# Moving a GRU state's transposes from TensorE to the DMA engines, with four groups of graphs under way

## The chip, the cores and the metric

One core of one Trainium2 chip. The metric is device time in microseconds (us), from the first to the last instruction of the kernel, of the slowest (here the only) core. The kernel before takes 2229.0 us (median of three runs, 2228.56 to 2229.5). The engines: TensorE (PE for matmuls, PEld for loading their stationary operand), VectorE (DVE), ScalarE (ACT), GpSimd (POOL) and SyncE (SP), whose queue issues all of the data transfers here.

## What is computed

128 graphs of 128 nodes with 256 features (`x`), and their adjacency (`adj`, about one edge in eight). Layer 0 is a gated graph network of three steps, layer 1 a graph attention; both stand behind a layer norm with ReLU and are added to their input.

```python
# layer 0
h = relu(layernorm(x))
A = (adj != 0)
for i in range(3):
    m    = h @ weight[i]
    aggr = einsum('bst,bsd->btd', A, m)            # sums over edges
    gi, gh = aggr @ w_ih.T + b_ih, h @ w_hh.T + b_hh
    r, z = sigmoid(i_r + h_r), sigmoid(i_z + h_z)
    n    = tanh(i_n + r * h_n)
    h    = (1 - z) * n + z * h
x = x + h
# layer 1
h  = relu(layernorm(x))
Wh = h @ W
s  = Wh.sum(-1)
e  = leaky_relu(s[:, :, None] + s[:, None, :], 0.2)
e  = where(adj == 0, -inf, e)
x  = x + softmax(e) @ Wh
```

## The kernel before

The 128 graphs go through in 32 groups of four. The weight of the messages is folded into `w_ih` beforehand, so a step of a group needs two products: of the state, and of its sums over the edges. They run in fp32. Each product of 2x2 blocks is done with seven block products in place of eight (the sums of blocks that this takes are `node_sums`). The sums over edges multiply the state, split into three bf16 parts whose sum is the fp32 value, with the 0/1 matrix in bf16: three passes.

A group's state is needed in two layouts. `hT` (features on partitions) feeds the gate products and holds the state in steps 0 and 1; `rows` (nodes on partitions) feeds the sums over edges and, in step 2, the gates, which come out in rows. TensorE turns one into the other by transposes into PSUM, and ScalarE copies the result to SBUF:

```python
def rows_to_T(src, dst):                 # once per group
    for k in range(KD):
        ps = buf("misc")
        def turn(k=k, ps=ps):
            for b in range(G):
                nc.tensor.transpose(flat(ps)[:, b * N:(b + 1) * N],
                                    ap(src)[:, b, k * P:(k + 1) * P], ident)      # L472
        op("PE", 440, turn, [src], [ps], [dst])
        op("ACT", 590, ... nc.scalar.copy(ap(dst)[:, k, :], flat(ps)) ...)        # L475

def T_to_rows(src, dst):                 # after steps 0 and 1
    for n in range(2):
        ps = buf("misc")
        def turn(n=n, ps=ps):
            for b in range(2):
                for k in range(KD):
                    nc.tensor.transpose(ap(ps)[:, b, k * P:(k + 1) * P],
                                        ap(src)[:, k, ...], ident)                # L486
        op("PE", 440, turn, ...)
        op("ACT", 590, ... nc.scalar.copy(ap(dst)[:, 2 * n:2 * n + 2, :], ap(ps)) ...)  # L490

def edge_sums(rows, a, dst):
    r1, p3 = buf("r1"), buf("p3")
    for n in range(2):
        # top() is the upper half of each fp32 number, read in place as bf16
        op("POOL", ... r1 = rows - top(rows))                                     # L505
        op("POOL", ... p3 = r1 - top(r1), written as bf16)                        # L508
    for k in range(KD):
        ps = buf("misc")
        # 4 graphs x 3 parts, bf16 matmuls with a                                 # L517
        op("ACT", 590, ... copy to dst ...)                                       # L521
```

[...] The state update of steps 0 and 1, and the end of step 2:

```python
# gru: VectorE, two SBUF inputs each
d = hT - u;  d = d * z;  hT = u + d              # L679, L682, L684
# gru_rows
op("DVE",  690, ... d  = rows - u)               # L717
op("POOL", 1290, ... x1 = xt + u)                # L719
op("DVE",  690, ... d  = d * z)                  # L722
op("DVE",  690, ... x1 = x1 + d)                 # L724
```

[...] A group:

```python
def group(g):
    xt, at, a = buf("xt"), buf("at"), buf("a")           # loads of x and adj
    rows, hT = buf("rows"), buf("hT")
    normed(xt, rows)
    rows_to_T(rows, hT)
    for layer in range(L):
        hs, aT, gs = buf("hs"), buf("aT"), buf("gs")
        node_sums(hT, hs, "POOL", 1290, 780)             # L546 to L550
        edge_sums(rows, a, aT)
        node_sums(aT, gs, "DVE", 690, 422)
        plan.phase = phase(g, layer)                     # 3 * g + 2 * layer, but for the last groups
        if layer < L - 1:
            gru(layer, hT, hs, aT, gs)
            rows = buf("rows")
            T_to_rows(hT, rows)
    gru_rows(L - 1, hT, hs, aT, gs, rows, xt, x1)
    attention(g, a, x1, h1, ...)
```

[...] The kernel does not issue in this order. Every operation is entered in a `Plan` with its engine and an assumed duration; a list scheduler then plays the engines through and fixes the order of each engine's queue before anything runs on the chip. The gate products of all turns (a turn is one step of one group, in the order of `phase`) form a fixed chain on TensorE; other work fills in around it. Tiles are `"set"` (one per group under way, `SETS = 3`), `"turn"` (given out in the order of turns), `"free"` or `"all"`. The assumed durations settle only the order; they say nothing of the chip.

Of the kernel before, what the change touches and what calls it, by code (L numbers as in the profile page):

```python
# [10 lines left out]
I32 = mybir.dt.int32  # L11
AF = mybir.ActivationFunctionType
# [3 lines left out]
P = 128  # L16
G = 4
EPS = 1e-5
ALPHA = 0.2
SETS = 3  # L20
SLOT = 18150
MARGIN = 4000
# [4 lines left out]
class Buf:  # L27


    def __init__(self, tag, key, prev):  # L30
        self.tag, self.key, self.prev = tag, key, prev
        self.slot, self.accesses, self.left = None, [], 0


class Plan:
# [7 lines left out]
    LAG = {"PE": 250, "ACT": 300, "DVE": 300, "POOL": 300, "SP": 2500}  # L43
# [20 lines left out]
    def op(self, eng, ns, fn, reads=(), writes=(), room=(), due=None, mark=None,  # L64
           turn=None):
# [14 lines left out]
        for is_write, group in ((False, reads), (True, writes)):  # L80
            for item in group:
# [4 lines left out]
                for x in list(reads) + list(writes)}  # L86
        free = [b for b in bufs.values() if self.tags[b.tag][1] in ("free", "turn")]
        for b in free:
            b.left += 1
        self.nodes.append([eng, ns, fn, deps, free, self.due if due is None else due])  # L90
# [7 lines left out]
    def run(self):  # L98
# [6 lines left out]
        bound = set(chain)  # L105
        rank = [0] * len(nodes)
        for i in reversed(range(len(nodes))):
            eng, ns, due = nodes[i][0], nodes[i][1], nodes[i][5]
            gap = 0 if i in bound else MARGIN
            rank[i] = min([due] + [rank[u] - (0 if nodes[u][0] == eng else self.LAG[eng])  # L110
                                   - (gap if u in bound else 0) for u in users[i]]) - ns
        missing = [len(n[3]) for n in nodes]
        for i, mark in self.turns:
            if mark in self.marks:
                users[self.marks[mark]].append(i)
                missing[i] += 1
        ready = {e: [] for e in self.LAG}
        at = [0.0] * len(nodes)
        for i, n in enumerate(nodes):
            if not missing[i]:  # L120
                ready[n[0]].append(i)
        clock = dict.fromkeys(self.LAG, 0.0)
        slots = {t: [0.0] * n for t, (n, kind) in self.tags.items()
                 if kind in ("free", "turn")}
        waiting = {t: [b for _, _, b in sorted(w, key=lambda x: x[:2], reverse=True)]
                   for t, w in self.waiting.items()}
        order, end = [], 0.0
        while len(order) < len(nodes):
            best = None
            for e, pool in ready.items():  # L130
# [3 lines left out]
                for i in pool:  # L134
                    if i in bound and i != chain[-1]:
                        continue
                    t = max(clock[e], at[i])
                    for b in nodes[i][4]:
                        if b.slot is None:
                            t = max(t, min(slots[b.tag]))  # L140
                            if b.tag in waiting and waiting[b.tag][-1] is not b:
                                t = float("inf")
                    starts.append((t, i))
# [11 lines left out]
            clock[e] = t + n[1]  # L155
            end = max(end, clock[e])
            for b in n[4]:
# [6 lines left out]
                b.done = max(getattr(b, "done", 0.0), clock[e] + self.LAG[e])  # L164
                if not b.left:
                    slots[b.tag][b.slot[1]] = b.done
            for u in users[i]:
                missing[u] -= 1
                at[u] = max(at[u], clock[e] + (0 if nodes[u][0] == e else self.LAG[e]))
                if not missing[u]:  # L170
                    ready[nodes[u][0]].append(u)
# [6 lines left out]
def kernel(  # L178
# [37 lines left out]
        "xt": (3, "all", work, [P, G, D]), "at": (1, "all", work, [P, G, N]),  # L216
        "a": (4, "all", work, [P, G, N]),
        "r1": (2, "free", work, [P, G, D]), "p3": (2, "free", work, [P, G, D]),
        "hT": (1, "set", work, [P, KD, GN]), "rows": (1, "set", work, [P, G, D]),
        "hs": (1, "set", work, [P, 4, H]), "aT": (1, "set", work, [P, KD, GN]),  # L220
        "gs": (1, "set", work, [P, 4, H]),
        "st": (8, "all", work, [P, G, 6]), "mv": (8, "all", work, [P, G, 2]),
        "rs": (8, "all", work, [P, G]), "nm": (8, "all", work, [P, G]),
        "s": (2, "all", work, [P, G]), "top": (2, "all", work, [P, G]),
        "den": (2, "all", work, [P, G]), "rden": (2, "all", work, [P, G]),
# [7 lines left out]
        "u": (2, "free", work, [P, G * D]), "d": (2, "free", work, [P, GN]),  # L233
        "x1": (2, "all", work, [P, G, D]), "h1": (1, "all", work, [P, G, D]),
# [10 lines left out]
    DTYPE = {"at": I32, "a": BF16, "p3": BF16}  # L245
# [92 lines left out]
    def weights():  # L338
        plan.due, plan.phase = 10 ** 9, -1
        w_hh_nat, w_ih_nat = buf("rz"), buf("rz")  # L340
        w_msg = [buf("h1"), buf("h1")]

        def load_msg(layer):
            op("SP", 1300, lambda: nc.sync.dma_start(
                ap(w_msg[layer // 2])[:, 2 * (layer % 2):2 * (layer % 2) + 2, :],
                weight[layer].rearrange("(k p) e -> p k e", p=P)),
               [], [(w_msg[layer // 2], layer, layer + 1)])
# [8 lines left out]
        load_msg(2)  # L356
# [14 lines left out]
        homes = [[last("hs"), last("gs")], [last("aT"), last("rows")], [last("hT"), buf("xt")]]  # L371
        for layer in range(L):
# [3 lines left out]
            wT, half, msg = uT[layer // 2], layer % 2, w_msg[layer // 2]  # L376
            for e in range(KD):
                ps = bank(layer == 0)

                def turn(ps=ps, e=e, msg=msg, half=half):  # L380
                    for k in range(KD):
                        nc.tensor.transpose(flat(ps)[:, k * P:(k + 1) * P],
                                            ap(msg)[:, 2 * half + k, e * P:(e + 1) * P], ident)
                op("PE", 220, turn, [(msg, layer, layer + 1)], [ps])
                to_sbuf("ACT", D, ps, wT, half * GN + e * D)
            w_x = homes[layer]
# [91 lines left out]
    def T_to_rows(src, dst):  # L478

        for n in range(2):  # L480
            ps = buf("misc")

            def turn(n=n, ps=ps):
                for b in range(2):
                    for k in range(KD):
                        nc.tensor.transpose(ap(ps)[:, b, k * P:(k + 1) * P],  # L486
                                            ap(src)[:, k, (2 * n + b) * N:(2 * n + b + 1) * N],
                                            ident)
            op("PE", 440, turn, [(src, n, n + 1), (src, 2 + n, 3 + n)], [ps], [dst])
            op("ACT", 590, lambda n=n, ps=ps: nc.scalar.copy(  # L490
                ap(dst)[:, 2 * n:2 * n + 2, :], ap(ps)), [ps], [(dst, 2 * n, 2 * n + 2)])

# [5 lines left out]
    def edge_sums(rows, a, dst):  # L498

        r1, p3 = buf("r1"), buf("p3")
        for n in range(2):
            part = slice(2 * n, 2 * n + 2)
            op("POOL", 1290, lambda part=part: nc.gpsimd.tensor_tensor(  # L505
                ap(r1)[:, part], ap(rows)[:, part], top(rows)[:, part], OP.subtract),
               [(rows, 2 * n, 2 * n + 2)], [(r1, n, n + 1)])
            op("POOL", 1290, lambda part=part: nc.gpsimd.tensor_tensor(  # L508
                ap(p3)[:, part], ap(r1)[:, part], top(r1)[:, part], OP.subtract),
               [(r1, n, n + 1)], [(p3, n, n + 1)])  # L510
        for k in range(KD):
            ps = buf("misc")

            def edges(k=k, ps=ps):
                for b in range(G):
                    for i, m in enumerate((top(rows), top(r1), ap(p3))):
                        nc.tensor.matmul(flat(ps)[:, b * N:(b + 1) * N],  # L517
                                         m[:, b, k * P:(k + 1) * P], ap(a)[:, b, :],
                                         start=(i == 0), stop=(i == 2))
            op("PE", 700, edges, [rows, r1, p3, a], [ps], [dst])  # L520
# [19 lines left out]
    def node_sums(t, w, eng, cost, half):  # L540
# [3 lines left out]
        def blocks():  # L544
            return ap(t).rearrange("p k (n m) -> p (k n) m", n=2)
        op(eng, cost, lambda: sub(ap(w)[:, 0:2, :], blocks()[:, 1::2, :], blocks()[:, 0:2, :],  # L546
                                  OP.subtract), [t], [(w, 0, 2)])
        op(eng, half, lambda: sub(ap(w)[:, 2, :], ap(w)[:, 1, :], blocks()[:, 0, :], OP.add),
           [t, (w, 1, 2)], [(w, 2, 3)])
        op(eng, half, lambda: sub(ap(w)[:, 3, :], blocks()[:, 2, :], ap(w)[:, 2, :], OP.subtract),  # L550
           [t, (w, 2, 3)], [(w, 3, 4)])
# [98 lines left out]
    def gru(layer, hT, hs, aT, gs):  # L650
# [7 lines left out]
        for j, n, src in blocks:  # L658
# [7 lines left out]
                op0=OP.add, op1=OP.mult), [nn, (rz, i, i + 1), W["bias_h"]], [(u, i, i + 1)])  # L666
            op("DVE", 422, lambda j=j, n=n, nn=nn: nc.vector.tensor_tensor(  # L667
                view(u)[:, j, n, :], view(u)[:, j, n, :], ap(nn)[:, 1, :], OP.add),
               [nn], [(u, i, i + 1)])
# [3 lines left out]
        for j in (1, 0):  # L673
# [7 lines left out]
               [(hT, lo, hi), (u, lo, hi)], [d])  # L681
            op("DVE", 690, lambda d=d, cols=cols: nc.vector.tensor_tensor(  # L682
                ap(d), ap(d), ap(rz)[:, 1, cols], OP.mult), [(rz, 4 + lo, 4 + hi)], [d])
            op("DVE", 690, lambda j=j, d=d, cols=cols: nc.vector.tensor_tensor(  # L684
                ap(hT)[:, j, :], ap(u)[:, cols], ap(d), OP.add), [(u, lo, hi), d], [(hT, lo, hi)])

    def gru_rows(layer, hT, hs, aT, gs, rows, xt, x1):
# [6 lines left out]
        for j, n, src in blocks:  # L694
# [10 lines left out]
               [nn, (rz, i, i + 1)], [(u, i, i + 1)])  # L705
            op("DVE", 422, lambda outs=outs, graphs=graphs, nn=nn: nc.vector.tensor_tensor(
                view(u)[:, graphs, outs], view(u)[:, graphs, outs], ap(nn)[:, :, P:2 * P], OP.add),
               [nn], [(u, i, i + 1)])
        for n in (1, 0):
# [3 lines left out]
            def part(b, lo=lo, hi=hi):  # L713
# [4 lines left out]
                ap(d), part(rows), ap(u)[:, cols], OP.subtract), [(rows, lo, hi), (u, lo, hi)], [d])  # L718
            op("POOL", 1290, lambda cols=cols, part=part: nc.gpsimd.tensor_tensor(  # L719
                part(x1), part(xt), ap(u)[:, cols], OP.add),  # L720
               [(xt, lo, hi), (u, lo, hi)], [(x1, lo, hi)])
            op("DVE", 690, lambda d=d, cols=cols: nc.vector.tensor_tensor(  # L722
                ap(d), ap(d), ap(rz)[:, 1, cols], OP.mult), [(rz, 4 + lo, 4 + hi)], [d])
            op("DVE", 690, lambda d=d, part=part: nc.vector.tensor_tensor(  # L724
                part(x1), part(x1), ap(d), OP.add), [d], [(x1, lo, hi)])

    def phase(g, layer):


        late = int(g == NG - 2 and layer > 0) - int(g == NG - 1)  # L730
        return 3 * g + 2 * layer + late

    def group(g):
        graphs = slice(g * G, (g + 1) * G)
        plan.due = (3 * g - 1) * SLOT
        xt, at, a = buf("xt"), buf("at"), buf("a")
        op("SP", 1500, lambda: nc.sync.dma_start(ap(xt), x[graphs].rearrange("b n d -> n b d")),
           [], [xt])
        op("SP", 800, lambda: nc.sync.dma_start(ap(at), adj[graphs].rearrange("b n m -> n b m")),
# [3 lines left out]
        plan.due = (3 * g + 6) * SLOT  # L743
        rows, hT = buf("rows"), buf("hT")
        normed(xt, rows)
        rows_to_T(rows, hT)
        for layer in range(L):
            hs, aT, gs = buf("hs"), buf("aT"), buf("gs")
            node_sums(hT, hs, "POOL", 1290, 780)
            edge_sums(rows, a, aT)  # L750
            node_sums(aT, gs, "DVE", 690, 422)
            plan.phase = phase(g, layer)
            plan.cursor = plan.phase * SLOT
            if layer < L - 1:
                gru(layer, hT, hs, aT, gs)
                rows = buf("rows")
                T_to_rows(hT, rows)
        plan.due = (3 * g + 7) * SLOT
        x1, h1 = buf("x1"), buf("h1")
        gru_rows(L - 1, hT, hs, aT, gs, rows, xt, x1)  # L760
# [114 lines left out]
```

## Time and profile before

| | before |
|---|---|
| time, us | 2229.0 (2228.56 to 2229.5) |
| TensorE, granted clock | 0.995 |
| TensorE matmuls | 13414 |
| gate matmuls, two queue entries of 256 columns, mean ns | 379 to 386 |
| GpSimd: splitting into bf16 parts (L505, L508), us | 209.8 + 197.9 |
| ScalarE: copies behind transposes (L490, L475), us | 74.4 + 37.7 |
| DMA, MB | 47.59 |

A group of the profile is one line of the program with one shape: line, engine, operation, output<-inputs, shape, count, then busy time and mean duration of one, then the time that the engine stood idle just before it and what it waited for. Durations on TensorE overlap, because a matmul is started while the one before it drains, so the distance between starts counts there. The names are those of the tiles in the program without their numbers: `misc` is one of two PSUM banks for everything but gates, `x_`, `y_` and `q_` are the gates' own banks, `t_rz` and `t_n` their copies in SBUF.

### The profile page before, as it was taken

How to read it: one execution, taken by the hardware profiler on the slowest of the kernel's cores; microseconds unless marked ns; L12 is line 12 of the kernel's file. 1: busy time of each engine (PE TensorE's matmuls, PEld its weight loads, DVE VectorE, ACT ScalarE, POOL GpSimd, SP SyncE). 2: the span in 40 equal slices, each digit the busy share in tenths (PEclk: the TensorE clock that was granted, in tenths of full speed). 3: DMA queues.
4: the chain of work that ended last, by engine and by line, in shares of the span. 5: the costliest groups of instructions: out<-in, count | busy, mean ns of one | idle time of the engine just before them, and what ended most of it. 6: DMA issues, size and time to landing. Idle time of an engine off the chain costs nothing. (4 is left out here: it accounts for less than half of the span.)

```text
span 2229.0 us, 34912 instructions
## 1 busy us (share of the span) xinstructions
PE 2201.2 (99%) x13414; PEld 1967.8 (88%) x13414; DVE 1623.3 (73%) x3330; ACT 1295.0 (58%) x2396; POOL 909.0 (41%) x889
## 2 busy tenths in 40 slices
PE   8999999999999999999999999999999999999996
PEld 6889998889998889998899988899988899988895
DVE  5587777877677877677777778776778776778667
ACT  4565656655656655566656566556566555666454
POOL 5354444343434343434344443434343434344321
PEclk9999999999999999999999999999999999999998
DMA  3000000000000000000000000000000000000000
GB/s 105 10 15 20 25 17 23 15 24 20 24 15 25 15 20 25 25 15 24 15 20 25 20 19 15 25 20 24 15 24 15 20 24 24 15 20 10 11 11 19
DMA packets 55671, 47.59 MB, mean 21 GB/s; under 512 B 3280, under 2 KB 55248, under 8 KB 55504
## 3 DMA queue, kind: packets, MB, share of 16 engines
q1 hardware_dynamic: 55504, 45.36, 6.5%
q8 instruction: 105, 1.72, 0.3%
q14 instruction: 62, 0.51, 0.1%
HBM read 28.58 MB, written 16.78 MB: 20 GB/s over the span
## 5 line engine op out<-in xcount | busy, mean ns | idle before, releaser
L546 POOL TENSOR_TENSOR hs<-hT 128x512 f32<-128x512 f32 x96 | 133.4, 1390 | 830.8 <-DVE hT L684 802.6
L616 DVE TENSOR_TENSOR t_rz<-t_rz,q_rz 128x512 f32<-128x512 f32 x192 | 131.6, 685 | 268.2 <-ACT t_rz L613 229.0
L613 ACT COPY t_rz<-y_rz 128x512 f32<-128x512 f32 x192 | 111.8, 583 | 318.7 <-PE y_rz L576 224.0
L719 POOL TENSOR_TENSOR x<-xt,u 128x512 f32<-128x512 f32 x64 | 84.8, 1324 | 357.6 <-ACT u L715 357.6
L505 POOL TENSOR_TENSOR r<-rows 128x512 f32<-128x512 f32 x192 | 209.8, 1106 | 38.2 <-ACT rows L490 27.2
L508 POOL TENSOR_TENSOR p<-r 128x512 bf16<-128x512 f32 x192 | 197.9, 1050 | 5.2
L576 PE MATMUL y_rz<-hs,s_hh 128*128 128x256 f32 x768 | 199.0, 381 | 0.0
L576 PE MATMUL y_rz<-gs,s_x 128*128 128x256 f32 x768 | 197.2, 379 | 0.0
L576 PEld LDWEIGHTS y_rz<-gs,s_x 128*128 128x128 f32 x768 | 145.7, 190 | 19.7
L576 PEld LDWEIGHTS y_rz<-hs,s_hh 128*128 128x128 f32 x768 | 138.9, 190 | 15.4 <-ACT t_rz L613 0.3
L616 DVE TENSOR_TENSOR t_n<-t_n,q_n 128x512 f32<-128x512 f32 x192 | 131.2, 683 | 13.4 <-ACT t_n L613 7.9
L517 PE MATMUL misc<-a,rows 128*128 128x128 bf16 x768 | 136.9, 219 | 0.1
L517 PE MATMUL misc<-a,p 128*128 128x128 bf16 x768 | 136.9, 219 | 0.0
L517 PE MATMUL misc<-a,r 128*128 128x128 bf16 x768 | 136.9, 219 | 0.0
L613 ACT COPY t_n<-y_n 128x512 f32<-128x512 f32 x192 | 112.6, 586 | 40.6 <-PE y_n L576 21.8
L576 PE MATMUL x_rz<-hT,s_hh 128*128 128x256 f32 x512 | 132.5, 381 | 3.1 <-DVE hT L684 3.1
L490 ACT COPY rows<-misc 128x512 f32<-128x512 f32 x128 | 74.4, 584 | 100.5 <-PE misc L486 96.9
L576 PE MATMUL x_rz<-aT,s_x 128*128 128x256 f32 x512 | 131.7, 380 | 0.0
L521 ACT COPY aT<-misc 128x512 f32<-128x512 f32 x192 | 111.5, 581 | 17.7 <-PE misc L517 14.1
L828 PE MATMUL misc<-w,uT 128*128 128x256 f32 x512 | 117.0, 381 | 0.3 <-ACT uT L537 0.2
L576 PE MATMUL y_n<-gs,s_x 128*128 128x256 f32 x384 | 115.8, 383 | 0.0
L676 ACT ACTIVATE u<-u,bias_i 128x512 f32<-128x512 f32 x128 | 92.5, 724 | 38.8 <-DVE u L667 38.8
(218 smaller groups left out, 6157.2 us busy)
## 6 DMA issues: line engine op xcount, KB each, us to landing
xt<-in_x_dram SPq DMA_DIRECT2D x32, 512.0 KB, 3.8
out_dram<-x SPq DMA_DIRECT2D x31, 512.0 KB, 3.0
at<-in_adj_dram SPq DMA_DIRECT2D x32, 256.0 KB, 2.9
rz<-in_L_gnn_w_ih_dram SPq DMA_DIRECT2D x1, 768.0 KB, 5.2
h<-in_L_gnn_weight_dram SPq DMA_DIRECT2D x3, 256.0 KB, 5.4
rz<-in_L_gnn_w_hh_dram SPq DMA_DIRECT2D x1, 768.0 KB, 8.1
out_dram<-x SPq DMA_DIRECT2D x2, 256.0 KB, 2.1
e<-in_L_gnn_b_ih_dram SPq DMA_DIRECT2D x1, 256.0 KB, 5.3
```

What stands on the lines that cost most here:

```text
L490: op("ACT", 590, lambda n=n, ps=ps: nc.scalar.copy(ap(dst)[:, 2 * n:2 * n + 2, :], ap(ps)), [ps], [(dst, 2 * n, 2 * n + 2)])
L505: op("POOL", 1290, lambda part=part: nc.gpsimd.tensor_tensor(ap(r1)[:, part], ap(rows)[:, part], top(rows)[:, part], OP.subtract), [(rows, ...
L508: op("POOL", 1290, lambda part=part: nc.gpsimd.tensor_tensor(ap(p3)[:, part], ap(r1)[:, part], top(r1)[:, part], OP.subtract), [(r1, n, n ...
L517: nc.tensor.matmul(flat(ps)[:, b * N:(b + 1) * N], m[:, b, k * P:(k + 1) * P], ap(a)[:, b, :], start=(i == 0), stop=(i == 2))
L521: op("ACT", 590, lambda k=k, ps=ps: nc.scalar.copy(ap(dst)[:, k, :], flat(ps)), [ps], [(dst, 2 * k, 2 * k + 2)])
L546: op(eng, cost, lambda: sub(ap(w)[:, 0:2, :], blocks()[:, 1::2, :], blocks()[:, 0:2, :], OP.subtract), [t], [(w, 0, 2)])
L576: nc.tensor.matmul(ap(bank)[:, half, :], ap(w)[:, i - 1, q, :], source(t, sums), start=(first and c == 0 and m == 0), stop=False, skip_gro ...
L613: op("ACT", 590, lambda: nc.scalar.copy(ap(t), ap(y)), [y], [t])
L616: op("DVE", 690, lambda: nc.vector.tensor_tensor(ap(t), ap(t), ap(q), OP.add), [q], [t])
L676: op("ACT", 723, lambda j=j, cols=cols: nc.scalar.activation(ap(u)[:, cols], ap(u)[:, cols], AF.Tanh, bias=ap(W["bias_i"])[:, 2 * KD + j:2 ...
L719: op("POOL", 1290, lambda cols=cols, part=part: nc.gpsimd.tensor_tensor(part(x1), part(xt), ap(u)[:, cols], OP.add), [(xt, lo, hi), (u, lo ...
L828: nc.tensor.matmul(ap(ps)[:, b, :], ap(uT)[:, k, (m + b) * N:(m + b + 1) * N], ap(w1)[:, k, :], start=(k == 0), stop=(k == KD - 1))
```

## The change

It takes the transposes of the state off TensorE and gives them to the DMA engines, which can transpose 2-byte elements. For that an fp32 state must be brought to 2-byte planes, which is done in two ways. Between rows and `hT` in full (into step 0, and into step 2) ScalarE packs the lower and the upper 16 bits of each number as two planes of integers, the DMA transposes the planes, and ScalarE packs them together again (`turned_halves`). For the sums over edges of step 1 only the three bf16 parts are needed in rows, so they are made from `hT` and turned as they are (`turned_parts`), and rows are not made at all. The first three groups still use TensorE for the first transpose.

A transfer takes longer to come back than a transpose on TensorE, so four groups are under way in place of three: the order of turns is now (g, 0), (g-1, 1), (g-2, 2), and between two steps of a group lie three turns of others instead of one. Room for it is made by giving `rows`, `hs`, `aT`, `gs` and the parts out by turns and by loading `x` a second time for the residual instead of keeping it.

The scheduler now counts operations of VectorE with two SBUF inputs (`two=True`) and all of GpSimd's as users of one port that run one after another. In the attention, the maximum is taken off inside exp (as its bias, bounded below) graph by graph, and the multiplication by the mask after exp is left out, since masked entries come out as zero already.

```diff
-SETS = 3
+SETS = 4
+EARLY = 3
-MARGIN = 4000
+MARGIN = 5000
[...]
-    LAG = {"PE": 250, "ACT": 300, "DVE": 300, "POOL": 300, "SP": 2500}
+    LAG = {"PE": 250, "ACT": 300, "DVE": 300, "POOL": 300, "SP": 4000}
[...]
+        self.nodes.append([eng, ns, fn, deps, free, self.due if due is None else due,
+                           two or eng == "POOL", self.LAG[eng] if lag is None else lag])
[...]
-                    t = max(clock[e], at[i])
+                    t = max(clock[e], at[i], port if nodes[i][6] else 0.0)
[...]
-        "xt": (3, "all", work, [P, G, D]), "at": (1, "all", work, [P, G, N]),
-        "a": (4, "all", work, [P, G, N]),
-        "r1": (2, "free", work, [P, G, D]), "p3": (2, "free", work, [P, G, D]),
-        "hT": (1, "set", work, [P, KD, GN]), "rows": (1, "set", work, [P, G, D]),
-        "hs": (1, "set", work, [P, 4, H]), "aT": (1, "set", work, [P, KD, GN]),
-        "gs": (1, "set", work, [P, 4, H]),
+        "at": (1, "all", work, [P, G, N]), "a": (6, "all", work, [P, G, N]),
+        "hT": (1, "set", work, [P, KD, GN]), "rows": (3, "turn", work, [P, G, D]),
+        "pl": (1, "turn", work, [P, 2, 3, GN]), "plT": (1, "turn", work, [P, 2, 3, GN]),
+        "r1": (1, "turn", work, [P, G, D]), "p3": (1, "turn", work, [P, G, D]),
+        "hs": (2, "turn", work, [P, 4, H]), "aT": (2, "turn", work, [P, KD, GN]),
+        "gs": (2, "turn", work, [P, 4, H]),
[...]
-    def T_to_rows(src, dst):
[...]
+    def turned_halves(src, rows, dst):
+        pl, plT = buf("pl"), buf("plT")
[...]
+        for k in range(KD):
+            op("ACT", 960, lambda k=k: nc.scalar.copy(
+                planes(pl, k), halves_of(src, rows)[:, k]), units, [(pl, k, k + 1)])
+            transpose(pl, plT, k, 2)
+            op("ACT", 960, lambda k=k: nc.scalar.copy(
+                halves_of(dst, not rows)[:, k], planes(plT, k)),
+               [(plT, k, k + 1)], units)
+
+    def transpose(pl, plT, k, n):
+        op("SP", 100, lambda: nc.sync.dma_start_transpose(
+            ap(plT)[:, k, 0:n].rearrange("p c (m q) -> p (c m) q", q=P),
+            ap(pl)[:, k, 0:n].rearrange("p c m -> p (c m)")), [(pl, k, k + 1)], [(plT, k, k + 1)],
+           lag=4500)
[...]
+    def turned_parts(hT):
+        pl, plT = buf("pl"), buf("plT")
[...]
+        for k in range(KD):
+            r = buf("d")
+            op("ACT", 620, lambda k=k: nc.scalar.copy(part(pl, k, 0), ap(hT)[:, k]), ...)
+            op("POOL", 1150, ... r = hT[:, k] - part(pl, k, 0))
+            op("ACT", 620, lambda k=k, r=r: nc.scalar.copy(part(pl, k, 1), ap(r)), ...)
+            op("POOL", 1150, ... part(pl, k, 2) = r - part(pl, k, 1))
+            transpose(pl, plT, k, 3)
[...]
-            op("POOL", 1290, ... part(x1), part(xt), ap(u)[:, cols], OP.add)
+            op("POOL", 1290, ... part(x1), part(x1), ap(u)[:, cols], OP.add)
[...]
+    turns = [(0, 0), (1, 0), (2, 0), (0, 1), (1, 1), (3, 0), (0, 2), (2, 1), (1, 2)]
+    for g in range(4, NG - 3):
+        turns += [(g, 0), (g - 1, 1), (g - 2, 2)]
+    turns += [...]
[...]
+            if layer == 0:
+                if g < EARLY:
+                    rows_to_T(rows0, hT)
+                else:
+                    turned_halves(rows0, True, hT)
+                parts = parts_of(rows0)
+            elif layer < L - 1:
+                parts = turned_parts(hT)
+            else:
+                rows, x1, h1 = buf("rows"), buf("x1"), buf("h1")
+                turned_halves(hT, False, rows)
+                parts = parts_of(rows)
+                op("SP", 100, ... x1 <- x[graphs])
[...]
-        op("DVE", cost, ... es(), es(), wide(top), OP.subtract)
-        op("ACT", 3200, lambda: nc.scalar.activation(es(), es(), AF.Exp), [], [e],
-           turn=(g + 2, 0, "n"))
-        op("DVE", cost, ... es(), es(), ap(a)[:, part], OP.mult)
+        op("DVE", 150, ... low = -max(top, -BIG / 1e3))
+        def exps():
+            for b in range(lo, hi):
+                nc.scalar.activation(ap(e)[:, b, :], ap(e)[:, b, :], AF.Exp, bias=ap(low)[:, b:b + 1])
+        op("ACT", 2600 + 390 * n, exps, [low], [e], turn=(g + 2, 1, "rz"))
```

## The prediction

> **What bounds the kernel now.** I read the page's busy line first, then busy time by stretch, then TensorE's own waits, then the timeline for what one instruction really costs, and the groups of instructions last.
>
> ```profile
> PE 2201.2 (99%) x13414; PEld 1967.8 (88%) x13414; DVE 1623.3 (73%) x3330; ACT 1295.0 (58%) x2396; POOL 909.0 (41%) x889
> ```
>
> TensorE is busy 99% of the span, no other engine over 73%. By stretch (length, then busy time of PE, PEld, DVE, ACT and POOL, granted clock, DMA share, GB/s):
>
> ```profile
> 0.00:20.00 20.00, 15.88 (x98) 12.45 (x98) 11.64 (x27) 10.38 (x21) 8.36 (x14) 1.00 0.89 230
> 20.00:40.00 20.00, 17.82 (x84) 15.38 (x84) 13.23 (x26) 10.94 (x21) 14.89 (x17) 1.00 0.20 60
> 40.00:100.00 60.00, 55.91 (x282) 44.39 (x281) 29.36 (x49) 26.25 (x52) 25.25 (x25) 0.94 0.00 1
> 100.00:1000.00 900.00, 900.00 (x5558) 809.90 (x5557) 666.63 (x1372) 533.75 (x987) 376.22 (x364) 1.00 0.07 21
> 1000.00:2000.00 1000.00, 1000.00 (x6134) 899.11 (x6133) 743.57 (x1534) 595.03 (x1099) 408.86 (x397) 1.00 0.06 20
> ...
> 2190.00:2229.00 39.00, 23.16 (x107) 18.02 (x106) 26.40 (x66) 13.86 (x23) 5.22 (x6) 0.82 0.08 28
> ```
>
> From 100 to 2000 us TensorE has no gap at the full clock. Its lost time lies at the ends: 4.1 + 2.2 + 4.1 us in the first 100 us, 15.8 us in the last 39. TensorE's waits say the same: the longest are single events of 2 to 3.5 us at start and end.
>
> ```profile
> PE misc L815 <- DVE e L805: 6.6, 2, 3.5
> PE misc L781 <- DVE hw L772: 3.2, 4, 2.6
> PE x_rz L576 <- DVE hT L684: 3.1, 1, 3.1
> ```
>
> So the middle is set by the sum of TensorE's issue times alone. A mean duration misleads there, as matmuls overlap; what one costs is the distance to the next start. In the timeline (start, length) four transposes are followed by a gate product:
>
> ```profile
> 1031.32 0.60 PE L486 MATMUL misc<-ident,hT 128*128 128x128 f32 x4
> 1031.76 1.03 PE L576 MATMUL y_rz<-hs,s_hh 128*128 128x256 f32 x4
> ...
> 1033.49 0.60 PE L486 MATMUL misc<-ident,hT 128*128 128x128 f32 x4
> 1033.92 0.60 PE L576 MATMUL y_n<-hs,s_hh 128*128 128x256 f32 x2
> ```
>
> Four start within 0.44 us, so a transpose costs 0.109 us of TensorE, not its mean of 0.275. The groups (instructions | busy us, mean ns | idle time before) give counts and the other engines' durations:
>
> ```profile
> L679 DVE TENSOR_TENSOR d<-hT,u 128x512 f32<-128x512 f32 x128 | 87.5, 685 | 3.8 <-ACT u L676 3.8
> ...
> L486 PE MATMUL misc<-ident,hT 128*128 128x128 f32 x512 | 77.1, 275 | 0.1
> ...
> L717 DVE TENSOR_TENSOR d<-rows,u 128x512 f32<-128x512 f32 x64 | 74.8, 1169 | 1.1 <-ACT u L715 1.0
> L490 ACT COPY rows<-misc 128x512 f32<-128x512 f32 x128 | 74.4, 584 | 100.5 <-PE misc L486 96.9
> ...
> L472 PE MATMUL misc<-ident,rows 128*128 128x128 f32 x256 | 38.6, 273 | 1.4 <-ACT hT L475 0.9 <-ACT u L316 0.5
> L537 ACT COPY uT<-misc 128x256 f32<-128x256 f32 x4 | 1.5, 372 | 5.2 <-PE misc L532 5.2
> ```
>
> **What the skill says.** "TensorE: Matmul & The Clock Gate", Part 4 (PE-mode transpose), gives some 275 ns for a transpose in a kernel's context and says that its result lands in PSUM, so that a copy must follow. The trace agrees on both: 275 ns mean, and L490 copies. The page's figure is the duration, though, and in this saturated engine the price is 109 ns. "Advanced Engine Details and Errata", X-Bar Transpose (TRN2), says that transpose DMAs are as fast as regular ones; no run so far shows one. This kernel's regular 256 KB load (adj) lands a median of 2.9 us after issue and its 512 KB load (x) 3.8 us, by the page's list of DMA issues. "SBUF — State Buffer", on engine ports, says that VectorE with two SBUF inputs and GpSimd hold one shared port pair exclusively, the loser blocking for the whole instruction. L717 shows it: 1169 ns where the same shape takes 685 in L679; GpSimd's L719 is released by the same tanh.
>
> **Part by part: TensorE.** All of L486 goes: 32 groups x 2 layers x 8 = 512 transposes x 0.109 = 55.8 us. L472 stays for the first three groups (EARLY), so (32 - 3) x 8 = 232 go: 25.3 us. Gates, edge sums (3 passes of bf16 as before) and attention's matmuls keep their counts; only their operands lie elsewhere. Sum: **81.1 us off the engine that sets the end**, and nothing added to it.
>
> **ScalarE.** Off: the copies behind those transposes, 74.4 us (L490) and 29/32 of L475's 37.7 = 34. Added: packing and unpacking of 16-bit halves, four copies of 1024 elements in each of 29 + 32 = 61 turns. From L490 and L537 a copy grows by (584 - 372) / 256 = 0.83 ns per element, so 1024 elements are about 584 + 512 x 0.83 = 1009 ns (an estimate: those read PSUM and fp32): 244 x 1.01 = 246 us. In the middle layer, four 512-element copies per group: 128 x 0.584 = 75. Exp split by graph: 31 x 0.63 (L803) becomes 128 x 0.32 (0.63 less 384 elements at 0.83 ns), +21. Net +234: 1295 becomes some **1529 us**, 71% of the new span, all beside TensorE.
>
> **VectorE.** The mask product after exp (L805, 36.3 us) and the subtraction of the maximum (L801, 22.8) go; a small negation comes (32 x about 0.17, like the reciprocal's 171 ns): 1623 becomes 1570. If the scheduler keeps GpSimd out of the way, up to 64 x (0.48 + 0.41 + 0.16) for L717, L722 and L724 (1169, 1106 and 864 ns against some 690 to 700) and 31 us for L796 and L797 go as well, some 98: between 1470 and 1570. None of it is on the path in the middle, so I count it at zero there.
>
> **GpSimd.** The splitting into three bf16 parts is done as often as before (on hT in one layer of three): about the same 909 us.
>
> **DMA.** Per turn two transposes, 256 KB each in 61 turns and 384 KB each in 32: 57.2 MB, and x read again for the residual, 16.8 MB. 47.6 becomes 121.6 MB, some 57 GB/s; the first 20 us ran at 230.
>
> **Latency.** A turn (one layer of one group) lasts (2190.6 - 17.7) / 96 = 22.6 us now, from the first gate product to the last. Today one other turn lies between two layers of a group, in the new list three, some 65 us. From the last product to the next layer's inputs I add: sigmoid 0.51, 0.48 + 0.42, tanh 0.72, 2.1 for three VectorE operations; parts 0.58 + 1.11 + 0.58 + 1.05; transfer 2.9 to 3.8; edge sums 0.67, copy 0.58, sums 1.6. About 14 us, 20 with the second half behind it. Even tripled it fits: the reason for four groups.
>
> **Sum.** 2229.0 - 81.1 = 2147.9. The 3.1 us wait on hT near 46 us should go, as three first layers now come before the first second layer (-4 with its neighbours), and the last attention is shorter by two operations of about 0.4 us in each of its two halves, less the longer exp (-2). **2142 us.**
>
> **Rivals.** *Transposing DMA as the bound.* There is one buffer each side ("pl", "plT"), so pack, two transfers and unpack must fit in one turn of about 22 us; above roughly 9 us per transfer they no longer do. At 12 us a turn would be 27 us and the kernel over 2500. For it: no trace here shows such a transfer. Against it: regular transfers of the size take 2.9 us, and the skill puts the two on a par. *ScalarE's queue turns into the wait.* It goes from 58% to 71%, with long copies ahead of short ones that free TensorE's banks; "misc" has two. If each of 96 turns loses 0.4 us, 38 us are given back: 2180, within 2%. Against it: VectorE at 73% leaves no gap today. *Early or late work.* Fewer "hs", "aT", "gs" and part buffers and three first layers at once could starve the start; some 10 to 20 us, once. *The port is the gain.* VectorE's up to 98 us of saved waiting would bring time only if TensorE waited for VectorE, and in the middle it never does.
>
> **Range and chances.** If the middle stays without gaps the time is 2148 less what the ends give back; they hold some 26 us of idle TensorE, of which I can't see more than 20 going: low 2128. The high end, 2175, allows about 0.3 us lost per turn or a worse start. A steady wait of over 0.4 us per turn, about one chance in eight, would bring it to the 2% line (2184) and beyond; slower than before by 2% needs the transposing DMA as the bound, about one in twenty.
>
> **What would show it.** Right: 13414 - 744 = 12670 matmuls, no row for hT transposes, L472's successor at x24; PE still without gaps between 100 and 2000 us; ScalarE near 1529 us; d<-rows,u near 690 ns; 121.6 MB moved; the span down by about the removed issue time. Wrong: PE waits at plT (late transfer) or at misc banks with ScalarE as releaser, repeated once per turn; transfers of 9 us or more; ScalarE well over 1600; or a first gate product much later than 17.7 us.

## The result, and the profile after

The changed kernel takes 2149.61 us (median of four runs, 2148.28 to 2153.59) against 2229.07 for the kernel before: ratio 0.9647, 95% interval 0.963 to 0.9663. Predicted were 2142 us, in a range of 2128 to 2175. All runs below are given as a ratio to the kernel before on the same chip.

The page's busy line of the changed kernel:

```profile
PE 2124.3 (99%) x12670; PEld 1894.7 (88%) x12670; DVE 1693.9 (79%) x3297; ACT 1543.7 (72%) x2675; POOL 948.4 (44%) x889
```

12670 matmuls, as counted beforehand: 744 fewer. TensorE is still at 99%, ScalarE went up as expected, VectorE against the expectation. By stretch (same columns as before):

```profile
0.00:20.00 20.00, 15.98 (x71) 12.37 (x72) 10.27 (x26) 8.71 (x18) 7.40 (x14) 1.00 0.84 250
20.00:40.00 20.00, 16.57 (x83) 13.73 (x82) 10.72 (x35) 9.11 (x19) 14.90 (x17) 0.83 0.35 104
40.00:100.00 60.00, 60.00 (x351) 51.51 (x350) 45.59 (x65) 39.89 (x79) 37.69 (x36) 1.00 0.24 45
100.00:1000.00 900.00, 898.66 (x5400) 803.49 (x5400) 721.06 (x1385) 665.02 (x1143) 402.07 (x374) 1.00 0.24 54
1000.00:2000.00 1000.00, 998.41 (x6006) 895.93 (x6005) 793.38 (x1549) 732.03 (x1261) 444.42 (x412) 1.00 0.26 57
...
2110.00:2152.00 42.00, 26.99 (x111) 20.79 (x109) 26.24 (x73) 13.65 (x29) 4.74 (x6) 0.78 0.11 38
```

The middle has 1.3 and 1.6 us of gaps where it had none; 40 to 100 us, which had lost 4.1 us, has none now. How much a group costs in the middle is read from one instruction that occurs once per group, the transposes of the attention's `s`, in the timeline of TensorE. First the kernel before, two lines that lie two groups apart:

```profile
1027.43 0.60 PE L781 MATMUL misc<-ident,s 128*128 128x128 f32 x4
...
1162.71 0.60 PE L781 MATMUL misc<-ident,s 128*128 128x128 f32 x4
```

then the changed one, three groups in a row, where long and short distances alternate:

```profile
1115.00 0.60 PE L891 MATMUL misc<-ident,s 128*128 128x128 f32 x4
1186.98 0.60 PE L891 MATMUL misc<-ident,s 128*128 128x128 f32 x4
1245.03 0.60 PE L891 MATMUL misc<-ident,s 128*128 128x128 f32 x4
```

Two groups took 135.28 us and take 130.03: 2.63 us less per group. The 24 transposes that a group no longer makes on TensorE are 24 x 0.109 = 2.62 us. That is the whole change of a group in the middle.

The list of DMA issues (count, KB, median us from issue to landing) and the new or changed groups of ScalarE and VectorE in the changed kernel:

```profile
rows<-in_x_dram SPq DMA_DIRECT2D x32, 512.0 KB, 4.3
at<-in_adj_dram SPq DMA_DIRECT2D x32, 256.0 KB, 2.9
plT<-pl SPq DMA_TRANSPOSE x186, 3.3
```

```profile
L758 DVE TENSOR_TENSOR d<-hT,u 128x512 f32<-128x512 f32 x128 | 110.5, 864 | 2.6 <-ACT u L755 2.6
L539 ACT COPY rows<-plT 128x1024 uint16<-128x1024 uint16 x64 | 82.2, 1338 | 0.0
...
L796 DVE TENSOR_TENSOR d<-rows,u 128x512 f32<-128x512 f32 x64 | 68.5, 1088 | 14.1 <-ACT u L794 14.1
L535 ACT COPY pl<-hT 128x1024 uint16<-128x1024 uint16 x64 | 64.3, 1046 | 1.8 <-DVE hT L763 1.8
```

A transposing transfer of 256 or 384 KB lands 3.3 us after its issue (median), between the regular transfers of 256 and 512 KB. On ScalarE, packing two planes takes 1046 ns, unpacking them 1338. On VectorE, L758 takes 864 ns where the same line took 685 before, and L796 is still at 1088.

### The profile page after: what moved, and what is told of

It reads as the page before. It is cut to its first block, busy times and chain, and to the rows that moved or that the text cites. A ratio compares the mean times of both kernels' runs of the same rounds, so it can differ in the third digit from the quotient of the medians.

```text
span 2151.8 us, 34116 instructions
## 1 busy us (share of the span) xinstructions
PE 2124.3 (99%) x12670; PEld 1894.7 (88%) x12670; DVE 1693.9 (79%) x3297; ACT 1543.7 (72%) x2675; POOL 948.4 (44%) x889
## 2 busy tenths in 40 slices
DMA packets 301750, 121.49 MB, mean 56 GB/s; under 512 B 232976, under 2 KB 301328, under 8 KB 301584
## 3 DMA queue, kind: packets, MB, share of 16 engines
q1 hardware_dynamic: 301584, 119.31, 24.5%
HBM read 45.36 MB, written 16.78 MB: 29 GB/s over the span
## 4 chain that ended last, share of the span: by engine, by line
PE 92%; DVE 5%; DMA 1%; ACT 1%; issue 1%; POOL 0%; DVEq 0%; ACTq 0%; POOLq 0%
PE y_rz L654 14%; PE q_rz L654 10%; PE x_rz L654 10%; PE y_rz L661 8%; PE y_n L654 7%; PE misc L596 6%; PE q_rz L661 5%; PE x_rz L661 5%; PE x_n L654 5%; PE q_n L654 5%; PE misc L930 5%; PE y_n L661 4%; PE x_n L661 3%; PE misc L610 3%; PE q_n L661 3%
## 5 line engine op out<-in xcount | busy, mean ns | idle before, releaser
L624 POOL TENSOR_TENSOR hs<-hT 128x512 f32<-128x512 f32 x96 | 128.8, 1342 | 326.3 <-PE y_n L661 275.9
L556 POOL TENSOR_TENSOR r<-rows 128x512 f32<-128x512 f32 x128 | 146.5, 1163 | 259.8 <-ACT rows L539 170.9
L654 PEld LDWEIGHTS y_rz<-hs,s_hh 128*128 128x128 f32 x768 | 144.3, 191 | 21.2 <-ACT t_rz L691 1.8
L628 POOL TENSOR_TENSOR hs<-hT,hs 128x256 f32<-128x256 f32 x96 | 75.0, 789 | 196.2 <-PE q_n L661 186.1
L559 POOL TENSOR_TENSOR p<-r 128x512 bf16<-128x512 f32 x128 | 155.5, 1233 | 0.3
L798 POOL TENSOR_TENSOR x<-x,u 128x512 f32<-128x512 f32 x64 | 84.8, 1341 | 157.9 <-DMA x<-in_x_dram 83.6
L576 POOL TENSOR_TENSOR d<-hT,pl 128x512 f32<-128x512 f32 x64 | 84.1, 1318 | 93.9 <-ACT pl L574 84.1
L930 PE MATMUL misc<-w,uT 128*128 128x256 f32 x512 | 122.8, 384 | 0.3 <-ACT uT L615 0.2
L654 PE MATMUL y_n<-hs,s_hh 128*128 128x256 f32 x384 | 114.5, 380 | 0.3 <-ACT t_n L691 0.2
L763 DVE TENSOR_TENSOR hT<-u,d 128x512 f32<-128x512 f32 x128 | 110.1, 862 | 3.5
```

What stands on the lines that cost most here:

```text
L556: op("POOL", 1106, lambda part=part: nc.gpsimd.tensor_tensor(ap(r1)[:, part], ap(rows)[:, part], top(rows)[:, part], OP.subtract), [(rows, ...
L559: op("POOL", 1050, lambda part=part: nc.gpsimd.tensor_tensor(ap(p3)[:, part], ap(r1)[:, part], top(r1)[:, part], OP.subtract), [(r1, n, n ...
L654: nc.tensor.matmul(ap(bank)[:, half, :], ap(w)[:, i - 1, q, :], source(t, sums), start=(first and c == 0 and m == 0), stop=False, skip_gro ...
L930: nc.tensor.matmul(ap(ps)[:, b, :], ap(uT)[:, k, (m + b) * N:(m + b + 1) * N], ap(w1)[:, k, :], start=(k == 0), stop=(k == KD - 1))
```

## The experiments

**Theory:** the gain is TensorE's issue time and nothing else; the four groups keep it, by hiding the latency. **Rivals:** the new order, the port rule or the shorter attention brought part of it; the DMA or ScalarE is near its limit.

| run | us | ratio (95%) |
|---|---|---|
| changed kernel | 2149.61 | 0.9647 (0.963 to 0.9663) |
| e1: all transposes on TensorE | 2236.87 | 1.0026 (1.0015 to 1.0037) |
| e2: only step 0 by DMA | 2208.07 | 0.9901 (0.9886 to 0.9915) |
| e3: three groups under way | 2203.44 | 0.9877 (0.9862 to 0.9892) |
| e4: no port rule | 2167.43 | 0.9716 (0.9702 to 0.9731) |
| e5: each transposing transfer twice | 2159.38 | 0.9679 (0.9665 to 0.9693) |
| e6: four times | 2660.51 | 1.1921 (1.1903 to 1.1939) |
| e7: kernel before with the port rule | 2258.44 | 1.0125 (1.011 to 1.014) |
| e8: old exp in the changed kernel | 2150.33 | 0.964 (0.9624 to 0.9656) |
| e9: changed kernel again | 2149.19 | 0.9634 (0.9621 to 0.9647) |
| e10: last group's end due earlier | 2149.45 | 0.9634 (0.962 to 0.9647) |
| e11: no port rule, VectorE booked later | 2148.14 | 0.9629 (0.9616 to 0.9642) |
| e12: three groups, VectorE booked later | 2280.54 | 1.0222 (1.0205 to 1.024) |

### Is it the transposes? e1 and e2

```diff
-EARLY = 3
+EARLY = 99                                   # e1 only
[...]
-                parts = turned_parts(hT)
+                rows = buf("rows")
+                T_to_rows(hT, rows)          # on TensorE, as before
+                parts = parts_of(rows)
[...]
-                turned_halves(hT, False, rows)
+                T_to_rows(hT, rows)
```

Expected of e1: 

> The changed kernel with its four groups, scheduler and attention, but all 768 transposes back on TensorE (no DMA transposes, no packing). If the gain is TensorE's issue time alone: 744 more transposes x 0.109 us = 81 us, so 2149.6 + 81 = 2231 us (2222 to 2240), within 2% of the kernel before. If the four groups, the port rule or the shorter attention brought part of the gain, it stays clearly below the kernel before: 2180 to 2210.

Expected of e2: 

> Only step 0 uses the transposing DMA; the state into steps 1 and 2 is turned by TensorE again, 512 transposes. If every transpose is worth 0.109 us wherever it stands: 2149.6 + 55.8 = 2205 us (2198 to 2212). If the gain hangs on one of the three places (for example because its wait sat near TensorE), it is off that line by over 10 us.

With all else of the change in place and the transposes back on TensorE the kernel is 0.3% *slower* than before. So the four groups, the port rule and the attention together bring nothing by themselves. In the middle e1 takes as long as the kernel before; two lines of its timeline, two groups apart:

```profile
1035.13 0.60 PE L908 MATMUL misc<-ident,s 128*128 128x128 f32 x4
...
1170.43 0.60 PE L908 MATMUL misc<-ident,s 128*128 128x128 f32 x4
```

That is 135.30 us for 135.28, so its 6 us over the kernel before lie outside this steady stretch, towards the start and the end. In e2, with 8 transposes of a group fewer than before, a group takes 66.77 us, 0.87 less: 8 x 0.109. The ratios of e1 and of the changed kernel (0.9634 to 0.9647 in its two measurements) are 0.038 to 0.039 apart, 85 to 87 us for the 81 expected; for e2 it is 57 to 60 us for the 55.8 expected. The gain goes by the number of transposes.

### How much the transfers bear: e5 and e6

```diff
     def transpose(pl, plT, k, n):
-        op("SP", 100, ... dma_start_transpose(plT, pl) ...)
+        for _ in range(2):                   # e6: 4; each waits for the one before
+            op("SP", 100, ... dma_start_transpose(plT, pl) ...)
```

Expected of e5: 

> The changed kernel with every transposing transfer made twice into the same place, the second waiting for the first: a transfer of 3.3 us becomes about 6.6. By the prediction's budget (pack, two transfers and unpack in one turn of 22 us; the limit is near 9 us a transfer) nothing changes: 2145 to 2160. If the transfers were already near their limit, or the latency between two steps were near the 65 us that four groups give it, the time rises by over 20 us.

Expected of e6: 

> The same with four transfers in a row, about 13 us for one half of the state. Above the limit of 9 us: two halves one after the other are 26 us for a turn of 22, so the transfers set the pace: 96 x 25 to 29 us, that is 2350 to 2800. If the halves overlap or three turns of slack absorb it, it stays within 30 us of 2150.

Twice the latency costs 0.3 to 0.5%, 7 to 10 us. TensorE's gaps between 100 and 1000 us grow from 1.3 to 6.1 us; between 1000 and 2000 us they stay at 1.5, so once the pipeline has settled twice the latency is free. Four in a row slow the kernel to 2660 us, within what was expected: some 82 us for a group in the middle. So the limit lies between two transfers in a row (about 7 us) and four (about 14); that it is 9 us is not shown. TensorE's waits in e6 (us in total, times, longest):

```profile
PE x_rz L655 <- ACT hT L539: 100.2, 26, 4.1
PE q_rz L655 <- POOL hs L625: 96.5, 27, 7.5
```

In nearly every group it waits once for the unpacked state and once for the sums made of a state. That is what late transfers look like here; the changed kernel shows neither wait. The 2660 us need not be the transfers' time alone, though: SyncE's queue, which issues the loads too, stood 227.3 us in all until the transfer before had landed, and the granted clock was 0.943 where the changed kernel had 0.994. How much each adds was not separated.

### Are four groups needed? e3 and e12

```diff
-SETS = 4
+SETS = 3
[...]
-    turns = [(0, 0), (1, 0), (2, 0), (0, 1), ...]
+    turns = sorted(..., key=lambda t: 3 * t[0] + 2 * t[1] + ...)   # the order before
[...]
-           turn=(g + 2, 1, "rz")
+           turn=(g + 2, 0, "n")
```

e12 has in addition `"DVE": 300` changed to `"DVE": 1200` in LAG, the time that the scheduler books between a result of VectorE and its use on another engine.

Expected of e3: 

> The changed kernel with three groups under way and the old order of turns, so that one turn (about 22 us) lies between two steps of a group instead of three. By my sum of the latency (14 us, 20 with the second half, before any queueing) it is near the limit: TensorE waits at the start of many turns, 1 to 5 us each, and the time goes to 2250 to 2600. The rival is that the latency is hidden by one turn anyway and four groups are not needed: 2145 to 2165.

Expected of e12: 

> Three groups with the old order of turns, as in the run that took 2203 us, and the scheduler booking 1.2 us after a VectorE operation. That run lost 0.9 us in every group at the same place (TensorE before a bank that ScalarE seeds late) and now and then some 2 us on a transposed plane. If nearly all of its 54 us are orders that don't fit, as without the port rule, it falls to 2150 to 2175; if one turn is too short for the latency, it stays at 2190 or gets slower, with TensorE waiting for transposed planes or for what is made of them.

Three groups give back 51 to 54 us of the gain. That is on the theory's side, but less than its least figure, and the waits are not those expected. TensorE's waits in e3:

```profile
PE q_rz L661 <- ACT q_rz L686: 15.7, 26, 2.1
PE misc L596 <- DMA plT<-pl: 9.3, 8, 1.9
```

A late transfer shows only eight times. The wait that comes with nearly every group is for ScalarE's seeding of a bank (0.5 us in this view; the gap in the starts is 0.65, and a group takes 65.9 us in place of 65.0). Over some 27 such groups that is about 25 of the 51 to 54 us; to the rest belong the late transfers, single waits of up to 4.3 us near the start, and a granted clock of 0.991 for 0.994. In the timeline ScalarE isn't waiting there: six operations without a pause stand ahead of L686 in its queue. e12 got slower, as was expected if one turn is too short, but not by the waits named for that: for transposed planes TensorE waits 2.3 us. With later bookings the same wait for a seed grew to the following:

```profile
PE q_rz L661 <- ACT q_rz L686: 71.1, 27, 2.8
```

So with three groups the largest single loss is an order on ScalarE, not the transfer. Both runs keep the port rule, which by itself cost the kernel before, also with three groups, 1.25% (e7 below); three groups without it were not tried. So it is not shown that four groups are needed, only that this scheduler finds no good order for three at either booking, while with four groups and without the rule it takes the later booking without loss (e11).

### The port rule: e4, e7, e11, and the old exp, e8

```diff
-                           two or eng == "POOL", self.LAG[eng] if lag is None else lag])
+                           False, self.LAG[eng] if lag is None else lag])      # e4 and e11
[...]
-    LAG = {"PE": 250, "ACT": 300, "DVE": 300, ...}
+    LAG = {"PE": 250, "ACT": 300, "DVE": 1200, ...}                            # e11 only
```

e7 is the kernel before with the rule (`two=True` on the same operations, and `port` in the scheduler's clock) and nothing else. e8 puts the two VectorE operations and the single exp back into the changed kernel.

Expected of e4: 

> The scheduler no longer knows the port that VectorE and GpSimd share; all else as in the changed kernel. Theory (TensorE alone sets the middle): 2149.6 within 6 us, whatever VectorE does. VectorE's busy time, 1694 us with the rule: if the rule keeps collisions down, it rises to 1720 to 1800; if the collisions come from GpSimd's work being ready at once, now that four groups are under way, and an order without a wait can't prevent them, it stays within 25 us of 1694. Rival for the time: more collisions delay TensorE's operands, 2170 or more.

Expected of e7: 

> The kernel before with the port rule alone (same instructions, another order). TensorE has no gaps in its middle, so there is nothing to gain: 2225 to 2233. VectorE's busy time shows whether the rule keeps collisions down where only three groups are under way: below 1600 us (1623 before) if it does. Rival: the rule is a gain in itself, worth some of the 17 us that its absence cost the changed kernel: 2210 to 2222.

Expected of e8: 

> The changed kernel with the old exp: the maximum subtracted and the mask multiplied by VectorE (two operations of 512 elements per group, some 59 us of VectorE in all), one exp for four graphs. Theory: VectorE's amount of work isn't what matters, as it waits elsewhere, so the time stays within 5 us of the changed kernel, with VectorE near 1750 us. Rival: as without the port rule, 60 us more of VectorE bring 10 to 20 us: 2160 to 2170.

Expected of e11: 

> Without the port rule as before, but the scheduler books 1.2 us instead of 0.3 between a VectorE operation and whoever uses its result, so an order no longer counts on VectorE being punctual. If the 1 us per group that the missing rule cost came from ScalarE standing behind a VectorE result that a collision made late, and not from the collisions as such, it goes: 2147 to 2156, with VectorE still above 1720 us busy. If collisions cost as such, it stays at 2162 to 2170.

e4 was expected to change nothing and cost 0.7 to 0.8%, 15 to 18 us. Its waits of TensorE begin with a line that the changed kernel has once, at 0.2 us:

```profile
PE y_rz L654 <- ACT t_rz L691: 15.7, 22, 0.7
```

One such place in e4's timeline, VectorE first, then GpSimd, ScalarE and TensorE:

```profile
1038.49 0.68 DVE L758 TENSOR_TENSOR d<-hT,u 128x512 f32<-128x512 f32 x1
1039.21 0.69 DVE L761 TENSOR_TENSOR d<-d,rz 128x512 f32<-128x512 f32 x1
1039.94 1.53 DVE L763 TENSOR_TENSOR hT<-u,d 128x512 f32<-128x512 f32 x1
```

```profile
1039.30 1.62 POOL L576 TENSOR_TENSOR d<-hT,pl 128x512 f32<-128x512 f32 x1 [4.25 <-ACT pl L574]
```

```profile
1041.50 0.62 ACT L574 CAST pl<-hT 128x512 bf16<-128x512 f32 x1 [1.79 <-DVE hT L763]
1042.03 0.58 ACT L691 COPY t_rz<-y_rz 128x512 f32<-128x512 f32 x1
```

```profile
1042.66 1.13 PE L654 MATMUL y_rz<-hs,s_hh 128*128 128x256 f32 x4 [0.73 <-ACT t_rz L691]
```

Read from the top: GpSimd's operation runs from 1039.30 to 1040.92; VectorE's L763, two SBUF inputs, is entered at 1039.94 and ends at 1041.47, 0.55 us after GpSimd's end, having taken 1.53 us instead of 0.69. "SBUF — State Buffer" of the Trainium skill (SBUF: two separate sides) says that whichever starts first holds the shared port pair for its whole instruction and that the other blocks. This agrees with it, within the roughness of GpSimd's spans. ScalarE stands at the cast that needs L763's result (1.79 us idle), and behind it in the same queue is the copy that empties TensorE's bank, for which nothing was missing. So TensorE waits 0.73 us, through an engine that had no part in the collision. It comes once per group.

e11 confirms the place, with a reservation. Later booking of VectorE's results, still without the rule, takes the loss away completely (0.9629); TensorE's waits for t_rz are down to 1.3 us, and L763 still takes 874 ns (886 in e4), so that operation collides as before and is merely no longer counted upon. But VectorE's busy time fell as well, from 1753.7 to 1704.7 us where over 1720 was expected, so the two causes are not wholly apart.

e7 shows the other side: in the kernel before, the rule does what it says, VectorE's busy time falls from 1623 to 1550.7 us and L717's successor to 696 ns, and the kernel is 1.25% slower. In e7's timeline one group's place:

```profile
1057.79 0.58 ACT L822 COPY eT<-misc 128x512 f32<-128x512 f32 x1
1058.43 2.05 PE L535 MATMUL misc<-eT,h 128*128 128x128 f32 x16 [0.68 <-ACT eT L822]
```

The new order puts a product on TensorE right behind the transposes whose copy it needs, and TensorE waits for ScalarE in every group (30 times, 20.4 us in the waits; the gap in its starts is 0.84 us, and a group takes 68.6 us instead of 67.6). VectorE and GpSimd have no part in these lines.

e8, finally, is the changed kernel within the error. VectorE's busy time was expected near 1750 us and came out at 1693.4, as in the changed kernel (1693.9): its other operations were held up less in sum (L758 took 746 ns for 864 and L763 776 for 862, though L796 took 1375 for 1088). So this run shows that the shorter attention is worth nothing to the time, but it didn't load VectorE more than before.

### The end: e9 and e10

```diff
-        plan.due = (phase(g, L - 1) + 3) * SLOT
+        plan.due = (phase(g, L - 1) + (3 if g < NG - 1 else 1)) * SLOT     # e10; e9 is unchanged
```

Expected of e9: 

> The changed kernel, run once more on the chip of the two beside it: 2147 to 2154 us.

Expected of e10: 

> The changed kernel with the due time of the last group's final operations two turns earlier in the scheduler, so that group 31's update and attention come before group 30's where both could run. In the middle nothing changes. In the end of the changed kernel, four-graph operations of the attention of group 30 (2.8 us on VectorE) and 3.5 us of its product on TensorE lie ahead of group 31's chain; if they sit on the path to the end, 3 to 7 us go: 2143 to 2148. If VectorE's total of the last 40 us (26 us) sets the end rather than the order, nothing is gained: within 2 us of the run beside it.

Nothing was gained. Beside e9, the last gate product of e10 ends 1.6 us earlier (2109.3 us for 2110.9), and what comes after it is 2.9 us longer (38.4 us for 35.5), with both groups' attention on VectorE and TensorE (TensorE waits 4.75 us for VectorE at 2119 us). No run beats the changed kernel by more than the error; e11, at 0.9629, is level with e9.

## Why the prediction was right, and where not

**TensorE's sum, right.** 81.1 us were to go. In the profiles the gate products run from 17.66 to 2194.6 us before and from 19.96 to 2115.8 after: 2176.9 and 2095.8 us, 81.1 less. Their start and end, two lines from the timeline of the kernel before and two of the changed one:

```profile
17.66 1.03 PE L576 MATMUL x_rz<-hT,s_hh 128*128 128x256 f32 x4
...
2193.98 0.61 PE L583 MATMUL q_n<-s_x,gs 128*128 128x128 f32 x4
```

```profile
19.96 1.03 PE L654 MATMUL x_rz<-hT,s_hh 128*128 128x256 f32 x4
...
2115.20 0.61 PE L661 MATMUL q_n<-s_x,gs 128*128 128x128 f32 x4
```

That this agrees to a tenth is chance: in e9's profile, where no stretch of the first 100 us has a lower clock (these two have one each, 0.94 and 0.83), the gate products run from 17.98 to 2110.9 us, 84.0 less than before. The 2.63 us per group don't hang on such single events.

Two readings in the prediction are loose, and nothing hangs on them. The last gate product ended at 2194.6 us, not at 2190.6, so a turn was 22.7 us, not 22.6. And the 275 ns of "TensorE: Matmul & The Clock Gate" (Part 4: PE-mode transpose) stand there behind a figure for bf16, while these transposes are fp32, so that the trace has 275 too need not confirm the page; the sum uses 0.109 us.

**The ends, wrong by some 8 us.** The step "-4 ... and -2" at the sum's end is the term that was mis-sized. The wait near 46 us did go, but others came in its place. The first gate product began 2.3 us later in the profiled run (17.98 in e9, so this is not the same in every execution), a wait for VectorE's gs lasted 3.42 us where it had lasted 2.17, the middle got some 3 us of gaps that it had not had, and what comes after the last gate product is 1.6 us longer, not shorter.

**ScalarE, right in sum.** 1544 for 1529 us. The estimate of 1009 ns from copies out of PSUM held for packing (1046) and failed for unpacking (1338): 279 us for both instead of 246; other groups came out shorter.

**VectorE, wrong.** "Between 1470 and 1570" became 1694, and "d<-rows,u near 690 ns" became 1088. The step that failed is "if the scheduler keeps GpSimd out of the way". The rule does avoid collisions: 72 us of VectorE's time with three groups (e7), 60 us with four (e4), but only 11 us beside e11, which books later without it. But it fixes an order, not moments, and with four groups more of them are left than with three: with the rule VectorE was busy 1634 us with three groups (e3) and 1694 with four. In the kernel before GpSimd's longest wait, 802.6 us in all, was for VectorE's last operation on hT, so it worked mostly when VectorE's chain was over; in the changed kernel that wait is no longer among its large ones. That this is how the collisions arose was not tried by itself. GpSimd's busy time grew too, from 909 to 948 us.

**"None of it is on the path", right for the time, but not for the reason given.** The operations saved on VectorE are indeed worth nothing (e8), yet its lateness can reach TensorE by way of ScalarE's queue. The fourth rival, that the port is the gain, is out by e7; that the rule doesn't matter to the time is out by e4, at the booking of the changed kernel; at the later one it doesn't (e11).

**Latency and DMA, right.** 121.49 MB for 121.6; transfers at 3.3 us, about a third of the 9 us that the budget allows. A limit exists (e6), between 7 and 14 us. "Advanced Engine Details and Errata" of the Trainium skill (X-Bar Transpose), which puts transposing and regular transfers on a par, is borne out for the time to landing at this size: 3.3 us between 2.9 and 4.3. It is not for the time on the DMA engines: the packets of the queue took 6.5% of the 16 engines' span for 45.36 MB before and 24.5% for 119.31 MB after, by which a transposed MB took about 1.8 times as long as a regular one (an estimate from these figures and the 57.2 MB transposed). With the engines taken for a quarter of the time, this is no limit here. That a turn of 22 us would be too short is shown for this scheduler only, with the port rule in it, and by another wait than the one I had in mind.

**ScalarE's queue as the wait, the second rival,** didn't come true in the changed kernel, but it is how e4, e7 and e12 lose most of their time, and e3 about half: t_rz behind a cast (e4), the bank's seed behind six others (e3), eT just ahead of its use (e7).

## What to carry to other kernels

When an engine has no gaps, price what you take off it by the distance between starts, not by durations: 0.109 us and not 0.275 per transpose gave the gain within a few us. Then look at what could stand between that engine and its operands in an in-order queue of another one: under a microsecond of lateness there, once per group, cost 15 to 18 us (e4), while the 59 us of operations saved on an engine with slack brought nothing (e8). Time taken off an engine can come back as latency and then needs work under way to hide it: with four groups the middle got 2.9 us of gaps, with three, in this scheduler, the kernel lost 51 to 54 us. And a fixed order hangs on what it counts upon: the later booking made the port rule unnecessary with four groups (e11), and made things worse with three (e12).

## What was not expected of the hardware

- In these copies of 16-bit integers on ScalarE it matters on which side the gaps are: reading every second half-word and writing densely took 1046 ns for 1024 elements (1043 from rows), reading densely and writing every second 1338, into rows and into hT alike.
- After a wait of 3.42 us near 28 us TensorE ran its next four gate matmuls in 2.07 us instead of 1.03, at a granted clock of 0.83 from 20 to 40 us; in e9 a wait of 3.29 us at the same place was followed by 1.13 us at 1.00. The same gap doesn't always cost the clock.
